# Second attention's probabilities and values as rows 124 to 127 of the text's keys and values, in a two-attention kernel on one core

## The chip, the core and the metric

The kernel runs on one core of a Trainium2 chip, in float32. The metric is the device time of one execution in microseconds (us). Below, PE is the matrix engine, DVE the vector engine, ACT the scalar engine, POOL the GpSimd engine, and SP the engine whose queue issues nearly all DMAs here.

## What is computed

The inputs are `x` (2 x 2048 x 640) and a context of 2 x 128 tokens of 384 channels. The first 124 tokens are text, the last 4 are called `ca`. There are 8 heads of 80 channels.

```
query = x @ Wq;  keyt = enc @ Wk;  valt = enc @ Wv          # 124 keys
hs = mha(query, keyt, valt)
ca_q1 = einsum('btc,th->bch', ca, Wq_ca)                      # 384 rows per batch
ca_q1 = ca_q1[:, linspace(0, 383, 2048).astype(int), :]       # 2048 rows, each row 5 or 6 times
ca_hs1 = mha(ca_q1, x, x)                                     # 2048 keys
ca_hs2 = mha(ca_hs1 @ Wq, ca @ Wk_ca, ca @ Wv_ca)             # 4 keys
out = (hs + ca_hs2) @ Wout + b_out + x
```

`mha` is softmax attention with the scale 80 ** -0.5. The second attention has only 384 different query rows per batch, since the 2048 rows repeat them in runs. Its last step has 4 keys: for each of the 384 rows and 8 heads there are 4 probabilities, `p2`.

## The kernel before, in words

**Order.** The work is written as tasks: Python generators that yield steps (`Do`) with an engine, a function, the events that it waits for, the buffers that it takes and frees, and the events that it marks. The tasks are started at lines 2151 to 2180. The literal `Desk.ORDER` (lines 74 to 152) lists task numbers; `Desk.run` (line 183) replays it, and each entry issues the next step of that task. A suffix a, v or g on an entry puts the step on ACT, DVE or POOL. Each engine and SP's queue execute in exactly this order, so an instruction that waits holds all that stand behind it on its engine.

**Helpers.** Nearly all matmuls have the profile's line L211 (`matmul`), warm-up matmuls L215, transposes L219, all operations of DVE, ACT and POOL L226, SP's DMAs L236, and the indirect additions L1971. `matmul` issues a product either whole (the row says 128*128) or as four strips of 32 output columns (128*32), which run beside each other. A float32 product takes two passes, so the profile counts 32 instructions for 16 strips.

**Stages.** Names in parentheses are those of the profile.

- Front: loads of x, Wq and the context; queries of block 0 (`queries`, line 1072, pq), keys (`keys`, line 800, pk), text values (`text_values`, pv into the tiles `vpad`, one per batch, 128 rows x 8 heads x 96), the second attention's values times Wout (`values_weights`, line 904, pw into w2_sb, with the bias b_out as its last row), and the table of row indices (`gather_rows`, line 859, query).
- Eight blocks of 512 rows of x: queries (`queries` while the block number is under FAST = 2, otherwise `queries_fast`, line 1173, which forms seven products of sums of x and Wq, x_sums and wq_sums), and the adapter's operands (`yz_block`, pyz).
- Adapter, once for each batch (`adapter`, line 1498): scores against 2048 rows (s), maxima on DVE (mx), exponentials on ACT (ea), and the contraction (`contract`, acc).
- Second attention, once for each batch (`second`, line 1657): the 384 x 8 x 4 probabilities are written into a padded tile (p2pad), turned on PE (pt_p), copied (p2T), multiplied with w2 (po<-w_sb,p2T, 6 products for each batch, copied to o2 by ACT) and stored as a 384 x 640 tensor in HBM (o<-o).
- Text attention in 16 units of 256 rows: scores (`text_scores`, sc, with the last query rows from a trip through HBM, first_rests and rests), softmax (p), a 32x32 transpose on DVE (eb), a trip through HBM (kept) from which pT comes back with the keys in its rows, in four parts of 32 rows (`probabilities`, line 1859), products with the values (`hidden`, ph), sums of those (hs) and products with Wout (`text_out_fast`, line 2004, po). Each po is added on DVE to the residual rows (x_more, last_rows), which were loaded from x (`residual`, line 1949) into one of eight row tiles.
- End of a row tile (`stored`, line 2117): once its four adds are done, POOL adds the rows of o2 to it by an indirect DMA with addition (`add_second`, line 1969), then it is stored. Units of batch 0 that are done before o2 is known are stored to HBM (early) and loaded again later. For the last unit the indirect addition is made ahead of the adds.

In rows 124 to 127 of `vpad` stand zeros, and pT's rows 124 to 127 hold the padding of p.

Of the kernel before, what the change touches and what calls it, by code (L numbers as in the profile page):

```python
# [8 lines left out]
F32 = mybir.dt.float32  # L9
# [7 lines left out]
T = 4  # L17
# [49 lines left out]
class Desk:  # L67
# [7 lines left out]
        2 2 2 2 0 4 4 108 109 110 2 2 0 0 0 0 0 0 0 0 0 2 2 2 2 2 0 4 4 0 4 2 2 0 0 37 111 113a 112a 4 4 0 0 115a 116a  # L75
        114v 4 6 6 6 5 5 6 6 6 2 16 16 16 16 16 16 16 5 3 6 16 16 13 11 11 7 5 3v 3 9 3a 6 6 7 117v 3 119v 3a 7 3 6 8
        118v 120v 1 9 8 8 6 122v 8 7 9 121 123a 124 7 8 7 7 8 7 126v 125v 6 7 7 127v 7 7 6 128a 129v 7 7 7 6 130a 131v
        132a 8 16 8 133 133 9 16 16 16 16 37 8 16 133 133 8 9 134 8 133 8 9 8 140 12 11 19 19 19 135 19 137 37 15 9 9
        9 9 15 15 15 15 15 15 15 136 9 136 136 136 9 15 15 19 19 19 19 19 136 19 10 18 9 9 9 138 9 10 13 18 12 18 37
        12v 12 13 18 18 12 37 15 37 143v 37 10 12 13 19 142v 19 19 19 19 18 37 13 37 12a 144a 9 145a 13 12 12a 146v 13  # L80
        14 102 102 107 136 136 141 141 141 141 141 6 136 136 107 139 18 18 37 40 18 37 37 147a 18 148 148 102 37 148
        148 102 102 102 139 139 22 139 139 22 22 22 22 22 139 17 17 149a 148 148 148 17 17 17 17 17 139 150 18 37 18
        44 18 18 150 17 17 150 37 17 17 151 102 37 150 22 22 22 18 18 151 37 148g 148 37 152a 151 151 150 139 139 151
        22 18 153 153 153 20 153 22 151 153 153 22 22 20 20 20 21 102 20 21 44 154 155 155 148 159g 160g 162g 161g 20
        158 158 151 151g 37 22 158 22 164 102 20 20 164 151 23 155 158 163 166 21 168a 163 166 37 169a 163 170a 171 20
        37 164 164 164 164 102 164 165 163 40 37 165 25 25 155 25 155 25 25 25 151 172a 20 173 173 20 174 37 164g 24
        158 173 173 155 155 173 173 164 21 23 37 167 156 23 23 155 164 48 37 175 173 173g 177 177 37 37 173 167 21 37
        167 177 155 177 177 177 48 37 177 21 37 178 179 179 23 157 25 157 157 157 157 157 25 25 158 180 21 25 24 37
        179 179 180 180 180 183g 177g 181g 182g 157 157 185 24 24 37 24 179 157 191a 185 180 179 192a 173 186 25 23 25
        23 177 180 187 187 187 187 193 177 52 179 37 25 37 195 195 37 24 185 179g 196 195 195 196 196 196 187 187 187  # L90
        196 25 179 179 197a 23 196 189 37 185 189 190 195 195 202a 195 37 25 203 56 204 195g 184g 205 23 205 195 37 37
        150 187 141 141 141 187 205 205 205 23 205 188 190 188 190 52 37 194 26 206 207 24 28 194 194 194 28 27 27 28
        28 195 28 194 28 28 28 28 158 23 208 205 213 214 37 37 214 27 208 208 208 208 217a 208 176 37 209g 211g 210g
        205g 205 218 28 141 205 176 141 215 37 215 216 219a 220a 208 208g 212g 37 176 28 56 28 221 28 221 208 37 213
        221 222a 221 221 216 213 216 37 37 223 213 221 221 224 28 28 30 194 194 194 194 30 176 198 199 176 158 208 150
# [144 lines left out]
def kernel(  # L240
# [30 lines left out]
    G = 32  # L271
    ONE = Y + T
    MAX = 4 * T
    VH = 2 * R
    VR = D - VH
    UNITS = B * NST // 2
    FAST, SPARE, IDLE = 2, 0, 14
    N2 = 3 * G + 2 * B * T

    desk = Desk(tc)  # L280
    matmul, transpose, copy, dma = desk.matmul, desk.transpose, desk.copy, desk.dma
    EITHER = ("ACT", "DVE")

# [1926 lines left out]
```

## Time and profile before

| | us |
|---|---|
| median of 3 runs | 583.91 |
| lowest and highest of the 3 | 580.39, 592.51 |
| the profiled execution's own time | 588.51 |
| its span in the profile | 586.7 |
| mean granted PE clock over the span | 0.988 |

The profiled execution is thus one of its own, 4.6 us above the median of the three runs. Busy times in it: DVE 394.1, ACT 265.8 and POOL 185.2 us; PE is shown with the prediction. The DMA engines move 115.27 MB, 196 GB/s in the mean, 10.69 MB of it on POOL's queue (the indirect additions and small loads).

How to read the rows: a group's row has the line, the engine, the operation, the tile written and the tiles read (buffer numbers left out), the partitions and elements, and the count; then the busy time in us, the mean duration of one in ns (on PE this is the latency, since matmuls are pipelined), and the engine's idle time just before them with what ended it. A row of the chain has the start, the duration in us, and the instructions that ran without a gap. A window's row has its length, then busy time and instructions of PE, PE's weight loads, DVE, ACT and POOL, then the granted PE clock (1.00 is full), the busy share of the DMA engines and GB/s.

### The profile page before, as it was taken

To read this page: it belongs to the slowest core of one execution; us is meant where nothing else is said; L and a number is where in the kernel's file an instruction comes from. 1 tells how busy PE (TensorE), PEld (TensorE's weight loads), DVE (VectorE), ACT (ScalarE), POOL (GpSimd) and SP (SyncE) were. 2 spreads that over 40 slices of the span, in tenths; PEclk is the share of its full clock that TensorE was granted. 3 is DMA by queue.
4 is the path that set the end of the run, shared out by engine and by line. 5 is a ranking of instruction groups with operands and counts; after the bars stand their busy time and mean duration, and the time that the engine had idled before them with its cause. 6 is when DMAs were issued, how large, how long until landed. Compare 5 with 4: busy or idle time off the path is not lost.

```text
span 586.7 us, 18285 instructions
## 1 busy us (share of the span) xinstructions
PE 572.0 (97%) x7769; PEld 307.1 (52%) x7769; DVE 394.1 (67%) x642; ACT 265.8 (45%) x738; POOL 185.2 (32%) x231
## 2 busy tenths in 40 slices
PE   9999899999999999999999999999999999997997
PEld 7563335546556645555454454555555565553453
DVE  2377799999997855579899999746334433652343
ACT  2011255555446788997344352585887411000100
POOL 7103051154232270012151335315323340442261
PEclk9999999999999999999999999997999999999799
DMA  8997585744898658445659989999868997999895
GB/s 273 173 249 153 110 165 138 164 122 141 155 247 166 204 153 184 118 135 159 194 166 192 260 259 247 243 248 250 235 177 204 216 239 224 216 214 232 258 201 171
DMA packets 153418, 115.27 MB, mean 196 GB/s; under 512 B 83317, under 2 KB 125685, under 8 KB 153338
## 3 DMA queue, kind: packets, MB, share of 16 engines
q1 hardware_dynamic: 147706, 103.42, 67.9%
q0 software_dynamic: 5632, 10.69, 10.7%
q8 instruction: 61, 1.00, 0.8%
q14 instruction: 19, 0.16, 0.1%
HBM read 72.54 MB, written 41.53 MB: 194 GB/s over the span
## 4 chain that ended last, share of the span: by engine, by line
PE 86%; DVE 6%; SPq 2%; ACT 2%; DMA 2%; issue 2%; DVEq 0%; ACTq 0%
PE po L211 28%; PE pq L211 23%; PE acc L211 7%; PE sc L211 7%; PE ph L211 6%; PE s L211 6%; SPq L236 2%; PE pyz L211 2%; DVE mx L226 2%; PE pk L211 1%; DMA xi<-in_x_dram 1%; PE unread L215 1%; DMA kept<-eb 1%; ACT ea L226 1%; ACT p L226 1%
## 5 line engine op out<-in xcount | busy, mean ns | idle before, releaser
L226 DVE TENSOR_REDUCE mx<-s 128x4 f32<-128x2048 f32 x48 | 109.0, 2271 | 4.8 <-PE s L211 4.7
L226 ACT ACTIVATE ea<-s 128x2048 f32<-128x2048 f32 x48 | 90.7, 1890 | 34.9 <-PE s L211 33.6
L226 ACT ACTIVATE p<-sc,m 128x124 f32<-128x124 f32 x256 | 89.9, 377 | 27.9 <-DVE m L226 27.7
L226 POOL TENSOR_TENSOR p<-p,r 128x992 f32<-128x992 f32 x25 | 48.8, 1954 | 157.9 <-DVE r L226 137.7
L211 PE MATMUL pq<-xt,wq_sb 128*32 128x256 f32 (+3 forms) x962 | 84.6, 427 | 0.1
L211 PE MATMUL po<-wout_sums,hs 128*32 128x320 f32 (+1 forms) x952 | 80.3, 442 | 0.0
L211 PE MATMUL po<-wout_sb,hs 128*32 128x320 f32 (+1 forms) x934 | 80.0, 438 | 0.2 <-ACT p L226 0.2
L226 DVE TENSOR_TENSOR x_more<-x_more,po 128x320 f32<-128x320 f32 x68 | 31.7, 479 | 54.8 <-PE po L211 54.7
L226 ACT ACTIVATION_READ_ACCUMULATOR p<-sc,m 128x1 f32 x256 | 56.1, 219 | 0.0
L226 ACT COPY hs<-ph 128x512 f32<-128x512 f32 (+1 forms) x27 | 14.7, 561 | 85.6 <-PE ph L211 85.5
L211 PEld LDWEIGHTS pq<-xt,wq_sb 128*32 128x32 f32 (+1 forms) x962 | 35.0, 113 | 33.9 <-issue 18.3
L211 PE MATMUL ph<-pT,vpad 128*32 128x256 f32 x768 | 48.1, 385 | 4.4 <-issue 4.4
L211 PEld LDWEIGHTS po<-wout_sb,hs 128*32 128x32 f32 (+1 forms) x934 | 34.7, 113 | 32.6 <-issue 2.9
L211 PE MATMUL acc<-ea,y_sb 128*32 128x384 f32 (+2 forms) x768 | 51.5, 389 | 0.0
L211 PEld LDWEIGHTS po<-wout_sums,hs 128*32 128x32 f32 (+1 forms) x952 | 34.4, 114 | 31.8 <-issue 3.1
L226 DVE TENSOR_REDUCE m<-sc 128x4 f32<-128x496 f32 x64 | 40.5, 659 | 10.9 <-PE sc L211 10.7
L226 DVE TENSOR_TENSOR last_rows<-last_rows,po 128x320 f32<-128x320 f32 x60 | 28.1, 481 | 28.3 <-PE po L211 27.8
L226 DVE STREAM_TRANSPOSE eb<-p 128x1024 f32<-128x1024 f32 x32 | 39.5, 1234 | 4.2 <-DMA kept<-eb 4.1
L1971 POOL DMA_INDIRECT last_rows<-o,query x16 | 25.1, 1570 | 53.7 <-DVE last_rows L226 50.6
L226 POOL TENSOR_TENSOR hs<-hs 128x256 f32<-128x256 f32 x32 | 26.8, 904 | 42.8 <-ACT hs L226 20.4
L211 PEld LDWEIGHTS sc<-kmain,q 64*128 64x128 f32 x512 | 32.4, 189 | 14.9 <-issue 8.8
L1971 POOL DMA_INDIRECT x_more<-o,query x16 | 25.6, 1599 | 45.2 <-ACT p L226 17.3
(210 smaller groups left out, 796.1 us busy)
## 6 DMA issues: line engine op xcount, KB each, us to landing
kept<-eb SPq DMA_DIRECT2D x32, 512.0 KB, 5.0
pT<-kept SPq DMA_DIRECT2D x64, 256.0 KB, 6.1
landing<-away SPq DMA_DIRECT2D x60, 128.0 KB, 3.4
xi<-in_x_dram SPq DMA_DIRECT2D x28, 256.0 KB, 4.6
x_more<-in_x_dram SPq DMA_DIRECT2D x17, 320.0 KB, 5.5
out_dram<-last_rows SPq DMA_DIRECT2D x16, 320.0 KB, 5.2
out_dram<-x_more SPq DMA_DIRECT2D x16, 320.0 KB, 5.2
last_rows<-in_x_dram SPq DMA_DIRECT2D x15, 320.0 KB, 4.9
```

What stands on the lines that cost most here:

```text
L211: self.pin(self.nc.tensor.matmul(out[strip], lhsT[:, strip], rhs, **kw))
L215: self.pin(self.nc.tensor.matmul(out, zeros, zeros, start=True, stop=True))
L226: return lambda *args, **kw: self.pin(getattr(engine, what)(*args, **kw))
L236: self.pin(self.nc.sync.dma_start(out, in_))
L1971: desk.pin(nc.gpsimd.indirect_dma_start(out=t, out_offset=None, in_=o2_of[b], in_offset=bass.IndirectOffsetOnAxis(ap=query[:, st : st + 1] ...
```

## The change

1. **Values.** `values_weights` becomes `second_values`: no transposes, no spreading, no product with Wout. The four values per head (vca) are copied from PSUM and written by eight small DMAs on SP into rows 124 to 127 of both vpad tiles (event "v2").
2. **Probabilities.** In `second`, the normalized p2 (p2t) is multiplied on PE with rows of 0 and 1 that POOL builds (`rows_of_tokens`, 3 memsets and 6 affine_selects for each batch): output column t takes the probabilities of the second-attention row that belongs to row t of x. The product has 32 rows (4 tokens x 8 heads) and 2048 columns, four groups of 512 side by side in one PSUM bank, in 6 matmuls. Two copies bring it to SBUF, one DMA on SP to HBM (p2, 256 KB, pieces of 128 bytes; event ("o2", b)).
3. **Text.** pT's last part has 28 rows in place of 32, and a fifth DMA on SP (`second_rows`, 32 KB) writes rows 124 to 127 from p2, for each of the 16 units. ph waits for all five parts and for "v2".
4. **What goes.** The index table, the o2 product with its copies, stores and 32 indirect additions, the early stores (4) and reloads.
5. **Bias.** b_out is loaded as a 128 x 640 tile; each of the 32 row tiles gets it by an addition of 128 x 640 before its po adds, 20 of them on POOL and 12 on DVE.
6. **Stores.** A row tile is stored after its four adds; those of the last unit in two halves of 320 columns.
7. **Front and order.** FAST goes from 2 to 1, so block 1's queries take the seven-product form. The first loads have another order (rows 0 and 1 of x, the first part of Wq, rows 2 and 3, the rest), and block 0's first query product is split into two halves of 256 columns. The key products have 248 columns in place of 256. 14 warm-up matmuls move from the first 9 us to just before the first sc. The whole literal `ORDER` is new: in it the first ph of a batch stands behind that batch's p2 product, where before the first ph stood ahead of the p2 transposes of batch 0.

On the engines this changes the number of instructions so: ACT loses 14 copies (o2, p2T) and those of w2; SP has 433 DMAs in place of 419; POOL's additions of two tiles in SBUF go from 57 to 81 (20 bias, 5 more of x_sums, 4 more of hs, the rest unchanged in kind), while its 32 indirect additions go.

The diff, without `ORDER` and cut to its core:

```diff
-    FAST, SPARE, IDLE = 2, 0, 14
+    FAST, SPARE, IDLE = 1, 0, 14
...
-    w2_sb = const.tile([N2 + 1, H], F32, name="w2_sb")
-    p2pad = const.tile([P, NCC, P], F32, name="p2pad")
-    query = const.tile([P, NST], mybir.dt.uint32, name="query")
+    bias = const.tile([P, H], F32, name="bias")
...
+        for op in (row(0), row(1), wq_rows(0), row(2), row(3)):
+            yield op
...
-                        pk[:, : B * NTOK], k_of(cc, c), ctxT[:, cc, :, :].rearrange("p b t -> p (b t)"),
+                        pk[:, : B * NK], k_of(cc, c), ctxT[:, cc, :, :NK],
...
-            dma(w2_sb[N2:, :], b_out[None, :])
+            dma(bias, b_out.partition_broadcast(P))
...
+        def away():
+            for b in range(B):
+                for g in range(4):
+                    k0 = G * g + T * b
+                    dma(vpad[b][NK:, 2 * g : 2 * g + 2, :], vca[k0 : k0 + T])
...
+        yield Do("SP", away, ["vca", "vpad"], marks=["v2"])
...
-            for i in range(NCH):
+            for u in range(2):
+
+                def part(u=u):
+                    for c in range(3):
+                        matmul(
+                            pq[c][:, 2 * P * u : 2 * P * (u + 1)], wq_of(0, c), t[:, 2 * u : 2 * u + 2, 0, :],
+                            start=(u == 0), stop=False, skip_group_check=True,
+                        )
...
+    def rows_of_tokens(b):
...
+            def steps(t=op.value[:, lo:hi], c=c, lo=lo, hi=hi):
+                desk.g_memset(t, 1.0)
+                for factor, base in ((1, NUM * lo - DEN * P * c), (-1, DEN * P * c - NUM * lo + DEN - 1)):
+                    desk.g_affine_select(
+                        out=t, in_=t, compare_op=ALU.is_ge, fill=0.0, base=base,
+                        pattern=[[factor * NUM, hi - lo]], channel_multiplier=-factor * DEN,
+                    )
...
+        def product(s):
+            pt = bank(s[0], f"pt_p2_{b}")
+            for g in range(4):
+                for c, (lo, hi) in enumerate(token_range):
+                    lo, hi = max(lo, 512 * g), min(hi, 512 * (g + 1))
+                    if lo < hi:
+                        matmul(
+                            pt[G * g : G * (g + 1), lo - 512 * g : hi - 512 * g],
+                            p2t[:, c].rearrange("p t h -> p (t h)"), by_token[b][0][:, lo:hi],
+                            start=True, stop=True, skip_group_check=True,
+                        )
+            return pt
...
+        p2_of[b] = hbm.tile([16, P, G], F32, tag=f"p2_{b}", name=f"p2_{b}")
+        yield Do(
+            "SP", lambda: dma(p2_of[b].rearrange("c p a -> p c a"), wide_p2.rearrange("p (c a) -> p c a", a=G)),
+            frees=[(eas, k)], marks=[("o2", b)],
+        )
...
+        def second_rows():
+            rows_in = p2_of[b].rearrange("(n c) (g t h) a -> g n t c (h a)", n=2, g=4, t=T)
+            dma(pT[NK:].rearrange("p i k h a -> p (i k) (h a)"), rows_in[n // 2, n % 2])
+
+        yield Do("SP", second_rows, [("o2", b)], marks=[("pT", m, 0)])
...
+        for k, (t, _, at) in enumerate(xr):
+
+            def add_bias(t=t):
+                (desk.g_tensor_tensor if desk.engine == "POOL" else desk.v_tensor_tensor)(t, t, bias, ALU.add)
+
+            yield Fork(one(Do(("DVE", "POOL"), add_bias, [at, ("wout", 2)], marks=[("xr", m, k)])))
...
-                "PE", product, [("pT", m), "v done"], needs=[(banks, 1)] + ([(hss, 1)] if c0 == 0 else []),
+                "PE", product, [("pT", m, j) for j in range(5)] + ["v done", "v2"], needs=[(banks, 1)] + ([(hss, 1)] if c0 == 0 else []),
...
-        if gather_last[m]:
-            op = yield Do("POOL", lambda: add_second(t, b, st), [*both, ("o2", b), "query"])
-            both = [op.at]
-        yield Do("SP", lambda: dma(rows_out, t), both, frees=[(rows, i)] + own)
+        cols = slice(0, H) if u == 2 else slice(u * HALF, (u + 1) * HALF)
+        yield Do(
+            "SP", lambda: dma(out[b, st * P : (st + 1) * P, cols], t[:, cols]), added,
+            frees=[(rows, i)] if u == 2 else [],
+        )
```

411 lines of the change are left out of this document (154 added, 257 removed).

## The prediction

> **What bounds the kernel now.** I read the page's busy table and chain first, then the list of what each engine waited for, then windows laid around the waits found, and last the SP queue's own timeline.
>
> ```profile
> span 586.7 us, 18285 instructions
> PE 572.0 (97%) x7769; PEld 307.1 (52%) x7769; DVE 394.1 (67%) x642; ACT 265.8 (45%) x738; POOL 185.2 (32%) x231
> ...
> PE 86%; DVE 6%; SPq 2%; ACT 2%; DMA 2%; issue 2%; DVEq 0%; ACTq 0%
> ```
>
> PE is busy 97% of the span and carries 86% of the chain, so only two things can move the end: PE work, and time in which PE waits or runs at half clock. The list of PE's waits is short:
>
> ```profile
> PE ph L211 <- issue: 4.4, 1, 4.4
> PE pv L211 <- DVE vpad L226: 2.5, 1, 2.5
> PE sc L211 <- DVE hs L226: 1.5, 1, 1.5
> ```
>
> Two of the three are followed by a slow clock (columns of a window: length, PE busy, ..., granted clock, DMA share, GB/s):
>
> ```profile
> 402.00:405.41 3.41, 3.41 (x34) 2.67 (x34) 1.43 (x3) 0.42 (x1) 2.61 (x2) 0.50 1.06 312
> 405.41:408.83 3.42, 3.42 (x36) 1.55 (x32) 0.49 (x2) 2.84 (x9) 0.00 (x0) 0.50 1.08 236
> 538.53:541.94 3.41, 0.46 (x8) 0.00 (x0) 0.33 (x1) 0.00 (x0) 0.00 (x0) 1.00 1.03 253
> 541.94:545.36 3.42, 1.96 (x20) 1.16 (x24) 0.00 (x0) 0.00 (x0) 0.00 (x0) 0.50 0.90 333
> 545.36:548.77 3.41, 3.41 (x28) 1.38 (x24) 0.82 (x2) 0.58 (x1) 0.72 (x1) 0.50 0.87 294
> ```
>
> Each slow stretch is two windows of 3.41 us at 0.50. In the first PE is busy throughout and loses 6.83 x 0.5 = 3.4 us. In the second it is busy 1.96 + 3.41 = 5.4 us and loses 2.7. With the waits themselves: 1.5 + 3.4 = 4.9 us near 400, and 4.4 + 2.7 = 7.1 us near 540.
>
> The wait near 540 is made by SP's queue (start, length; POOL's timeline, SP's, then the chain):
>
> ```profile
> 517.11 1.54 POOL L1971 DMA_INDIRECT x_more<-o,query  x1 [0.30 <-issue]
> ...
> 527.40 0.83 SPq L236 DMA_DIRECT2D out_dram<-x_more  x2
> 534.78 0.34 SPq L236 DMA_DIRECT2D x_more<-in_x_dram  x1
> 535.17 0.43 SPq L236 DMA_DIRECT2D pT<-kept  x1
> ...
> 538.99 4.42 issue
> 543.40 1.94 PE ph L211 x16
> ```
>
> Finished rows get their second-attention part by two indirect additions (POOL, the second until 518.7), and only at 527.40 are they stored. The next row load takes their place at 534.78, the last part of pT is queued behind it at 535.17, and the ph product starts at 543.40.
>
> **PE work removed.** Prices are rows of the chain (start, us, count) and of the groups by form:
>
> ```profile
> 32.55 1.72 PE pq L211 x4
> 42.69 1.30 PE pk L211 x6
> 68.51 1.08 PE pw L211 x16
> 453.65 1.73 PE ph L211 x32
> 470.43 10.24 PE po L211 x38
> 504.74 12.92 PE po L211 x192
> ...
> L211 PE MATMUL po<-w_sb,p2T 113*32 113x320 f32 x72 | 6.6, 438 | 0.0
> L211 PE MATMUL po<-w_sb,p2T 113*128 113x320 f32 x6 | 2.1, 432 | 0.0
> L219 PE MATMUL pt_p<-ident,p2pad 128*113 128x128 f32 x6 | 1.0, 283 | 0.1
> ```
>
> A strip of 320 columns costs 12.92/192 = 67 ns, a full product 10.24/38 = 269 ns. The o2 products go: 72 x 67 + 6 x 269 = 6.5 us. The two pw products go, 16 strips each: 32 x 67.5 = 2.2. The p2 transposes with those of the values: 0.9. The first block's key products shrink from 256 to 248 columns, 30 full-size equivalents x 217 x 8/256 = 0.2.
>
> Block 1's queries become the seven-product form that other blocks have. Plain they are 25 products, each of two passes at 430 ns, 21.5 us. The new form has 56 + 16 passes over 256 columns at 216.5 (1.73/32 = 54 for a strip, as ph's) and 10 of 512 at 430: 19.9. That saves 1.6.
>
> Added are two p2 products of 32 rows, each some 2048 columns in four 32-row strips. Side by side a strip of 512 costs 430/4 = 108 ns a pass, so 0.9 us a product; one behind another 3.4. I take 0.9 twice, as the strips in these rows run side by side: 1.7. Sum: -6.5 - 2.2 - 0.9 - 0.2 - 1.6 + 1.7 = **-9.7** (-4.6 if serial).
>
> **The stall near 540.** Without an indirect addition a row's store needs only DVE's adds, and x_more's were done before the second indirect addition began, 10 us ahead of 527.40. Row loads and pT parts then stop queueing behind it: **-7.1**. What is late next is the fifth part of pT, below, but there it was available long before.
>
> **Other engines.** POOL loses 32 indirect additions (half of them in the first row) and gets bias additions, priced by the second:
>
> ```profile
> L1971 POOL DMA_INDIRECT last_rows<-o,query x16 | 25.1, 1570 | 53.7 <-DVE last_rows L226 50.6 <-issue 1.5 <-DMA last_rows<-early 1.4
> L226 POOL TENSOR_TENSOR wout_sums<-wout_sb,wout_sums 128x640 f32<-128x640 f32 x2 | 3.1, 1556 | 0.2
> ```
>
> Of 32 bias additions POOL has 20 at 1.56 us, 31 us; DVE has 12. POOL's 0/1 rows are two sets of nine operations over some 680 columns, at most 1.56 each by the same row, and need nothing of p2. POOL at 32% and DVE at 67% have the room in the sum, so I take 0 for it; the cover is that rows are loaded well ahead of their po sums. Without that cover one late addition costs PE 1.56. ACT loses 14 copies and gains 4. The indirect additions, the o2 tensor and the early rows (some 14 MB by their sizes) leave the DMA engines: 0 while PE is not short of data, and a gain only inside the waits below.
>
> **New waits.** Every ph product now waits for a fifth part of pT, and that for p2 (DMA issues with us to landing; one tile's instructions with ns min/median/max):
>
> ```profile
> pT<-kept SPq DMA_DIRECT2D x64, 256.0 KB, 6.1
> landing<-away SPq DMA_DIRECT2D x60, 128.0 KB, 3.4
> xi<-in_x_dram SPq DMA_DIRECT2D x28, 256.0 KB, 4.6
> z<-zs SPq DMA_DIRECT2D x8, 256.0 KB, 3.2
> away<-first_rests SPq DMA_DIRECT2D x2, 256.0 KB, 3.2
> first_rests<-away SPq DMA_DIRECT2D x4, 128.0 KB, 3.3
> ...
> L226 ACT CAST first_rests<-pq x2: 374/376/378, 41.1 to 42.1; 128x256 fp32r<-128x256 f32 x2
> L226 ACT CAST rests<-first_rests x2: 619/620/622, 70.0 to 70.5; 128x512 fp32r<-128x512 f32 x2
> ```
>
> The chain behind the p2 product: two ACT copies of 256 columns, 0.8; the 256 KB store, between 3.2 (z<-zs) and 4.6 (xi, 128-byte pieces); the 32 KB load, between 3.3 and 6.1. That is 7.3 to 11.5; I take 7.5 to 8.5, as the load is small. Before its own first ph the new instruction order has 5.2 us of PE work for batch 0 (scores, yz) and 6.0 for batch 1: **+2.2** (0 to 5) and **+2.4** (0 to 7; batch 1 falls where DMA is over 0.9). Behind a waiting fifth part on SP stand the next row loads and stores, so this wait is not refunded elsewhere.
>
> At the start, the first sc in the new order stands directly behind the values' products, where before block 1's queries stood between. It needs the first block's last query rows: evacuation 0.8, store 3.2, load 3.3, two casts 1.2 = 8.5 us. Beside it lies 5.4 us of PE work, and ahead of the load SP has about 3 us of other issues (eight small value parts among them). That is a wait of 6, less the 2.5 at pv that it covers: **+4** (0 to 7). The warm products, moved there from the start, fill this idle time and add none.
>
> Half clock behind these waits: of the three waits shown two drew a slow stretch. One of 3.4 us with even odds: **+1.7** (0 to 7). The rule beside these rows is in the Trainium skill, "TensorE: Matmul & The Clock Gate", Part 1: the clock is halved after at least one idle window of about 3.4 us. The trace's slow windows have that length, but the one at 402 followed only 1.5 us of idle. By the rule, none of waits this short would slow the clock, and the sum would be 575.3.
>
> **The tail.**
>
> ```profile
> 583.22 0.33 SPq L236 DMA_DIRECT2D out_dram<-x_more  x1
> ```
>
> The span ends 3.5 us behind the issue of the last store of 320 KB. The last unit is now stored in halves; its gain lies between 0 and 0.5 (landing's 128 KB took 3.4 as well, z<-zs 3.2), I take **-0.3**.
>
> **Sum**: -9.7 - 7.1 + 2.2 + 2.4 + 4 + 1.7 - 0.3 = -6.8. The profiled execution took 588.5, so it would be 581.7; that execution is 4.6 above the median of 583.9, so the forecast against the median is 577.1, put at 577.0.
>
> **The rivals.** (a) The new waits are hidden. The chain times are medians of a loaded DMA system, now 14 MB lighter, and 5.2 to 6 us of cover stands against 7.5. Then only -9.7 - 7.1 - 0.3 = -17.1 counts: 566.8. Against it: z<-zs alone took 3.2 from issue to landing, twice in a row that is 6.4 without copies.
>
> (b) Slower. One mechanism: POOL's additions hold up DVE's sums of two SBUF tiles.
>
> ```profile
> 398.23 3.02 DVE L226 TENSOR_TENSOR hs<-hs 128x256 f32<-128x256 f32 x1 [0.20 <-ACT hs L226]
> ...
> 398.52 2.44 POOL L226 TENSOR_TENSOR p<-p,r 128x992 f32<-128x992 f32 x1
> ```
>
> This hs sum took 3.02 us beside a POOL addition, and PE's sc waited for it: the 4.9 us near 400. Such POOL additions rise from 57 to 81. From 577.0 to the 2% bound at 595.6 is 18.6 us, four such events that reach PE; it gives 597. Against it: one of 32 sums reached PE before. The Trainium skill, "SBUF — State Buffer", section "Who interferes with whom", says a DVE instruction with two SBUF inputs and a GpSimd one that reads SBUF lock each other out for a whole instruction; the 3.02 agrees.
>
> (c) Batch 1's adapter chain, not PE, sets when p2 is known. Then the 9 us of PE work saved before it turn into a wait at its first ph, and with that wait's 2.4 in it: 577.0 + 9 - 2.4 = 583.6. For it: DVE, which has the score maxima mx, is on the chain at 6%. Against it, PE's waits for mx:
>
> ```profile
> PE s L211 <- DVE mx L226: 0.4, 2, 0.2
> ```
>
> **How the numbers follow.** My forecast 0.53, (a) 0.27, (c) 0.14, (b) 0.06. The bounds of 2%, about what a measurement tells from no change, are 572.2 and 595.6. Faster: most of (a), 0.25, and 0.05 of the forecast's low end, 0.30. Slower: (b), 0.06. Same: 0.64. The range 566 to 588 leaves out (b), the lower part of (a) and a little of (c). The likeliest case by itself spans 570 to 585.
>
> **What would show it.** L1971 gone from the groups; no PE idle time near the end. A PE wait of 2 to 3 us before the first ph of each batch, ended by a DMA into pT; none means (a). A wait of 3 to 6 us before the first sc. PE busy down by 9 to 12 us. hs sums on DVE of 2 us and more beside POOL's additions mean (b). A gap at batch 1's p2 product that DVE ends means (c). I am wrong on the sum if the slow stretches are more than two, or if a wait appears where none of these parts puts one.

## The result and the profile after

The kernel after takes **592.88 us** (median of 20 runs, 587.82 to 596.48) against 583.45 (20 runs) for the kernel before: ratio 1.0165, 95% interval 1.0134 to 1.0197. It is slower by 9.4 us; I had forecast 577.0, 6.5 faster. The profiled execution took 594.39, 1.5 above the median.

The page of the kernel after (span, busy times, shares of the chain):

```profile
span 592.5 us, 18520 instructions
PE 562.9 (95%) x7934; PEld 308.1 (52%) x7934; DVE 405.7 (68%) x643; ACT 262.3 (44%) x729; POOL 181.9 (31%) x208
...
PE 77%; DVE 12%; DMA 5%; issue 2%; ACT 2%; SPq 2%; ACTq 0%; DVEq 0%
```

PE is busy 9.1 us less, as forecast (9 to 12), and yet the span is 5.8 longer: PE's share of the chain fell from 86% to 77%, and DVE's and DMA's rose. PE waits more. PE's longest waits in the kernel after:

```profile
PE pt_x L219 <- DMA xz<-in_x_dram: 5.6, 2, 4.1
PE ph L211 <- DMA pT<-p: 5.0, 1, 5.0
PE sc L211 <- ACT rests L226: 4.6, 1, 4.6
PE po L211 <- DVE x_more L226: 3.1, 2, 3.0
PE ph L211 <- issue: 2.9, 1, 2.9
PE s L211 <- DVE mx L226: 1.8, 2, 1.2
```

The first is the start, where the warm products stood before. The two waits at ph (batch 0, batch 1) and that at sc are those that I had named. The one at po, 3.0 us, nobody had. Windows of the kernel after tell what they cost; the first three are all its stretches at half clock in which PE works:

```profile
65.70:72.53 6.83, 4.21 (x40) 2.52 (x44) 6.59 (x9) 3.52 (x16) 3.63 (x3) 0.50 1.02 194
318.29:321.70 3.41, 2.73 (x28) 1.58 (x32) 0.00 (x0) 0.58 (x1) 1.84 (x2) 0.50 0.49 115
328.53:335.36 6.83, 5.74 (x44) 2.16 (x48) 4.82 (x8) 2.09 (x10) 2.09 (x2) 0.50 0.83 188
300.00:340.00 40.00, 32.08 (x420) 16.27 (x420) 29.03 (x38) 12.28 (x46) 16.75 (x13) 0.87 0.72 168
480.00:520.00 40.00, 36.94 (x576) 21.49 (x572) 23.04 (x43) 5.05 (x20) 7.27 (x7) 1.00 0.77 197
520.00:580.00 60.00, 60.00 (x944) 30.39 (x940) 27.43 (x57) 4.04 (x8) 18.77 (x18) 1.00 0.54 151
```

and the last three of the kernel before:

```profile
300.00:340.00 40.00, 39.59 (x535) 20.70 (x527) 39.66 (x49) 16.05 (x63) 14.71 (x14) 1.00 0.89 217
480.00:520.00 40.00, 40.00 (x623) 20.15 (x625) 18.70 (x36) 4.06 (x9) 14.65 (x13) 1.00 0.82 211
520.00:580.00 60.00, 55.58 (x824) 28.28 (x820) 23.10 (x52) 3.96 (x8) 21.28 (x16) 0.94 0.97 231
```

The end is as forecast: from 520 to 580 PE has no idle time and the full clock. Most of the loss is from 300 to 340: PE is busy 7.5 us less there, and of its busy time 2.73 + 5.74 us ran at half clock, which loses half of them, 4.2 us: 11.7 in all. From 480 to 520 it is 3.1.

What happens from 305 to 336 is seen in the timelines of the kernel after: SP's queue, then PE, then DVE (start, length, what; in brackets the idle time ahead and what ended it):

```profile
309.56 0.38 SPq L236 DMA_DIRECT2D p<-rows  x1
...
312.69 0.43 SPq L236 DMA_DIRECT2D pT<-kept  x1
...
313.83 0.46 SPq L236 DMA_DIRECT2D pT<-p  x1
...
321.14 0.43 SPq L236 DMA_DIRECT2D z<-zs  x1
...
307.65 1.07 PE L211 MATMUL pt_p<-rows,p2t 128*32 128x512 f32 x12
318.97 3.25 PE L211 MATMUL ph<-pT,vpad 128*32 128x256 f32 x32 [4.95 <-DMA pT<-p]
...
329.62 4.50 PE L211 MATMUL po<-wout_sums,hs 128*32 128x320 f32 x32 [2.95 <-DVE x_more L226]
...
327.78 0.01 DVE L226 LOAD_MASK_SELECT zs<-yz  x1 [2.66 <-DMA z<-zs]
...
329.00 0.47 DVE L226 TENSOR_TENSOR x_more<-x_more,po 128x320 f32<-128x320 f32 x1
```

The store of p2 (p<-rows) is issued at 309.56, the fifth part of pT (pT<-p) at 313.83, with six other DMAs issued in between, and ph begins at 318.97, 10.3 us behind the end of the product (308.72). Behind that, z<-zs is issued only at 321.14; DVE, which works in its own order, waits 2.66 us for it and adds x_more behind it; PE's po waits 2.95 us for that addition. Both waits are followed by slow PE work: 32 products take 3.25 and 4.50 us, where the same take 1.93 and 2.36 in no_block below.

What SP's queue itself waited for, in two stretches of the kernel after (300 to 330, 470 to 490):

```profile
SPq L236 <- ACT rows L226: 9.0, 1, 9.0
...
SPq L236 <- DMA away<-wq_sums: 4.0, 1, 4.0
...
SPq L236 <- ACT rows L226: 5.8, 1, 5.8
SPq L236 <- DMA out_dram<-x_more: 4.5, 1, 4.5
SPq L236 <- DMA p<-rows: 1.9, 1, 1.9
```

"ACT rows" is the copy of p2 from PSUM. SP reached the store 9.0 us (batch 0) and 5.8 us (batch 1) before that copy was made, and until then it issued nothing.

The 4.0 us follow from the 9.0. The store of wq_sums (away<-wq_sums) stands behind the store of p2 and was issued at 313.21, against 308.10 in no_block; the part of pT at 318.89 waits until it has landed, and z<-zs stands behind that part. Its data was there at 317.01, so SP held z<-zs back by 4.1 us. From its issue until DVE went on it then took another 6.6 us (2.5 in no_block), beside what SP had issued just ahead of it.

### The profile page after: what moved, and what is told of

The parts are those of the page before. It is cut to its first block, busy times and chain, and to the rows that moved or that the text cites. A ratio compares the mean times of both kernels' runs of the same rounds, so it can differ in the third digit from the quotient of the medians.

```text
span 592.5 us, 18520 instructions
## 1 busy us (share of the span) xinstructions
PE 562.9 (95%) x7934; PEld 308.1 (52%) x7934; DVE 405.7 (68%) x643; ACT 262.3 (44%) x729; POOL 181.9 (31%) x208
## 4 chain that ended last, share of the span: by engine, by line
PE 77%; DVE 12%; DMA 5%; issue 2%; ACT 2%; SPq 2%; ACTq 0%; DVEq 0%
PE po L211 25%; PE pq L211 19%; PE acc L211 7%; PE ph L211 7%; PE sc L211 6%; PE s L211 6%; DVE mx L226 5%; SPq L236 2%; PE pyz L211 1%; PE pv L211 1%; DMA z<-zs 1%; PE pk L211 1%; DVE xt L226 1%; DMA xz<-in_x_dram 1%; DMA away<-wq_sums 1%
## 5 line engine op out<-in xcount | busy, mean ns | idle before, releaser
L226 DVE TENSOR_REDUCE mx<-s 128x4 f32<-128x2048 f32 x48 | 109.4, 2278 | 10.4 <-PE s L211 10.1
L226 POOL TENSOR_TENSOR p<-p,r 128x992 f32<-128x992 f32 x25 | 46.6, 1863 | 157.0 <-DVE r L226 157.0
L211 PE MATMUL po<-wout_sums,hs 128*32 128x320 f32 (+1 forms) x940 | 80.7, 445 | 3.1 <-DVE x_more L226 3.1
L211 PE MATMUL po<-wout_sb,hs 128*32 128x320 f32 (+1 forms) x970 | 78.9, 433 | 0.0
L211 PE MATMUL pq<-xt,wq_sb 128*32 128x256 f32 (+3 forms) x936 | 75.7, 402 | 0.0
L226 POOL TENSOR_TENSOR hs<-hs 128x256 f32<-128x256 f32 x36 | 28.2, 792 | 132.0 <-DVE hs L226 91.3
L211 PE MATMUL ph<-pT,vpad 128*32 128x256 f32 x768 | 47.9, 388 | 7.8 <-DMA pT<-p 5.0
L211 PEld LDWEIGHTS po<-wout_sums,hs 128*32 128x32 f32 (+1 forms) x940 | 35.4, 115 | 36.1 <-issue 3.7
L211 PEld LDWEIGHTS pq<-xt,wq_sb 128*32 128x32 f32 (+1 forms) x936 | 36.9, 117 | 28.3 <-issue 11.9
L211 PEld LDWEIGHTS po<-wout_sb,hs 128*32 128x32 f32 (+1 forms) x970 | 34.6, 111 | 31.3 <-issue 1.7
L211 PE MATMUL acc<-ea,y_sb 128*32 128x384 f32 (+2 forms) x768 | 49.6, 382 | 0.0
L226 ACT COPY hs<-ph 128x512 f32<-128x512 f32 (+1 forms) x24 | 12.3, 528 | 66.6 <-PE ph L211 66.6
L211 PEld LDWEIGHTS ph<-pT,vpad 128*32 128x32 f32 x768 | 25.9, 112 | 24.9 <-issue 10.8
L211 PE MATMUL pq<-xt,wq 128*32 128x512 f32 x308 | 38.8, 596 | 0.0
L211 PEld LDWEIGHTS sc<-kmain,q 64*128 64x128 f32 x512 | 31.1, 187 | 11.4 <-issue 9.2
```

Source lines behind the costliest of these rows:

```text
L211: self.pin(self.nc.tensor.matmul(out[strip], lhsT[:, strip], rhs, **kw))
L226: return lambda *args, **kw: self.pin(getattr(engine, what)(*args, **kw))
```

## The experiments

Four causes stood against one another: the wait of ph for p2's trip through memory (theory 1 in the expectations); POOL and DVE burdened by bias additions (rival (b), theory 2); the wait at the first sc (theory 3); and SP's queue, which the store of p2 holds up in order, with all that stands behind it (theory 4). In `ORDER`, 310 and 443 are `second` of batch 0 and 1, 311 and 444 `rows_of_tokens`, 68 and 88 the first text units of the two batches, 140 the first rests, 11 the small loads of values. Ratios are to the kernel before, in runs of the same chip. In kernels with a changed `ORDER` the lines are one lower (L210 for L211).

### Is it the dependence on p2, the additions, or the front?

**rows_free**: no unit waits for p2; the fifth part is a load of x of the same size, so the output lacks the second attention.

```diff
-            rows_in = p2_of[b].rearrange("(n c) (g t h) a -> g n t c (h a)", n=2, g=4, t=T)
-            dma(pT[NK:].rearrange("p i k h a -> p (i k) (h a)"), rows_in[n // 2, n % 2])
+            rows_in = x[b, : T * HEADS, : HEADS * R].rearrange("(t c) k -> t c k", t=T)
+            dma(pT[NK:].rearrange("p i k h a -> p (i k) (h a)"), rows_in)
```

> The changed kernel, except that the fifth part of pT is read from x, which is there from the start, so no ph product waits for p2 (the second attention's share of the output is left out; the DMA keeps its size and its place in SP's queue, and p2 is still made and stored). Theory 1 (the trip of p2 through memory is what costs): the waits of 5.0 us at 313.5 and 2.9 us at 484.3 go, with the half clock behind the first (about 1.7 us) and part of the 3.0 us wait at 326.2 that follows it; 581 to 585 us, ratio to the kernel before 0.995 to 1.002. Theory 2 (the bias additions on POOL and DVE cost): these waits are only filled by others, at most 4 us less, 589 us or more. Theory 3 (the front is what costs): 588 to 590.

591.59 us, ratio 1.0135 (1.0085 to 1.0184). Two rows, one of what SP's queue waited for, one of PE's waits, in rows_free:

```profile
SPq L236 <- ACT rows L226: 9.0, 1, 9.0
```

```profile
PE ph L211 <- DMA pT<-in_x_dram: 5.5, 1, 5.5
```

The fifth part, now a plain load of x, came as late as before (4.2 us behind the store's issue, 4.3 in the kernel after), since SP still stood 9.0 us at the store. The dependence alone is not the cause.

**no_bias**: no bias is added, and the output lacks it.

```diff
-            yield Fork(one(Do(("DVE", "POOL"), add_bias, [at, ("wout", 2)], marks=[("xr", m, k)])))
+            yield Fork(one(Do(("DVE", "POOL"), lambda: None, [at, ("wout", 2)], marks=[("xr", m, k)])))
```

> The changed kernel without the 32 additions of the bias tile (the bias is left out of the output; every other instruction keeps its place). Theory 2: the 3.0 us wait at 326.2 goes with its half clock of 2.2 us, and smaller delays of DVE and POOL with it; 583 to 587 us, ratio 1.000 to 1.006. Theories 1 and 3: 591 to 594 us, ratio 1.013 to 1.018, as the additions lie beside PE work and the wait at 326.2 comes from the SP queue and the mask shuffle that waits for it on DVE.

592.79, 1.0158 (1.0105 to 1.0212), with the same waits. Rival (b) falls. Its own sign, hs sums on DVE of 2 us and more, is missing in the kernel after, too: there is none, where the kernel before had the one of 3.02 us.

**front_sp**: the small loads of values stand behind the loads of the first rests.

```diff
-  18 9 11 9 139 ... 135 106 140 0 140 141 140 140 140 18
+  18 9 9 139 ... 9 9 140 140 140 140 140 11 9 144v ... 135 106 0 141 18
```

> The changed kernel with one edit of the order: the trip of the first block's last query rows (store, the returns of the key parts, loads of first_rests) stands ahead of the eight small value DMAs in SP's queue. Theory 3: these eight issues (5.2 us) are what the first sc waits for; its wait falls from 4.6 us to under 1, and the half clock behind it (about 2 us) goes; 586 to 589 us, ratio 1.004 to 1.010. If the values' rows, now later, hold up the tiles that take the place of the front's (yt, rests), the time stays at 592 to 594. Theories 1 and 2 say that PE only waits elsewhere: 590 to 593.

593.77, 1.0177 (1.0129 to 1.0225). In its profile the wait for the rests was 0.6 in place of 4.6, with full clock behind it, and the span 1.6 shorter; the median did not fall. The front is not where the 9 us are.

**before_again**: the kernel before, unchanged, for another profiled execution.

> The kernel before, unchanged, for a second profile. The 20 runs have a median of 583.5 us against 588.5 of the profiled one. If the two stalls that the prediction priced (7.1 us near 540, 4.9 us near 400) belong to every run, they show again. If they are events of that one execution, one or both are missing here and the time is 579 to 585 us; then the 7.1 us that the prediction took off was never there to be had.

584.58 us, span 582.8. A window and the wait behind it in before_again:

```profile
520.00:580.00 60.00, 56.16 (x868) 31.64 (x860) 24.69 (x56) 3.85 (x8) 21.40 (x16) 1.00 0.96 238
```

```profile
PE ph L211 <- issue: 3.0, 2, 2.6
```

The stall near 540 is there, but 2.6 us long and with no half clock. The 7.1 us that I had removed in the forecast were 4.4 and 2.7 in one execution, not in all. The hs sum near 400 again takes 3.09 us and PE waits 1.5 us for it, this time with no half clock behind it.

### The queue, and the dependence with it

**no_block**: rows_free, and the two stores of p2 (310, 443) stand later in SP's order, where their data exists. The output again lacks the second attention.

```diff
-        yield Do("SP", second_rows, [("o2", b)], marks=[("pT", m, 0)])
+        yield Do("SP", second_rows, [], marks=[("pT", m, 0)])
...
-  276 105 310 233 286 ... 34 286 335 341 ... 458 443a 443 88 88 ... 465v 80 451 80
+  276 105 233 286 ... 34 286 310 335 341 ... 458 443a 88 88 ... 465v 80 443 451 80
```

> As rows_free (the fifth part of pT read from x, so the second attention's share of the output is left out), and the store of p2 stands later in SP's queue, behind the parts of pT and the row loads that it stood ahead of. Theory 4: what ph waits for at 313.5 and 484.3 is the SP queue itself, since the store of p2 stands in it 9.0 and 5.8 us before its data is there and holds the last part of pT, the landing loads and the row loads behind it. Then both waits go here though they stayed in rows_free, with the half clock behind the first and the 3.0 us at 326.2: 10 to 14 us less than the changed kernel, 579 to 583 us, ratio 0.992 to 1.000. Rival (the adapter's maxima on DVE set the pace there, and PE would wait for them instead): the wait at 313.5 falls to under 1 us, but the time only to 588 to 590, ratio 1.008 to 1.012.

**580.21** (12 runs), ratio 0.9944 (0.9911 to 0.9977): 12.7 us under the kernel after. PE's timeline in no_block:

```profile
315.90 1.93 PE L210 MATMUL ph<-pT,vpad 128*32 128x256 f32 x32 [0.34 <-ACT yz L225]
...
322.92 2.36 PE L210 MATMUL po<-wout_sums,hs 128*32 128x320 f32 x32 [0.45 <-DVE x_more L225]
...
475.32 1.94 PE L210 MATMUL ph<-pT,vpad 128*32 128x256 f32 x32
```

The three waits are 0.34, 0.45 and nothing, and the wait at po, which has nothing to do with p2, went with them. The wait at the first sc (4.2) is still there. So the loss lies in p2's way through memory: the wait for it, and what it holds up.

### Whole computation, other orders on SP

Six kernels keep everything and only move entries of `ORDER`. **early_p2**: batch 0's shares and product 2.4 us earlier, its store behind the last part of pT; batch 1's product earlier too.

```diff
-  68 286 314a 245 295 245 307 306 274 310 317a 312 310 312 245 ... 311 311 311 310 310a ... 105 310 233 ... 456 461 444 444 444 443 456
+  68 286 310 314a 245 295 310 245 307 306 274 317a 312 312 311 311 311 310 245 ... 310a ... 105 233 ... 276 68 310 318 ... 80 88 444 444 444 443 452
```

> The whole computation of the changed kernel, with p2 known earlier: for batch 0 the probabilities are divided ahead of one maximum on DVE and the p2 product stands two query products earlier on PE (2.4 us), and its store behind the last part of pT in SP's queue; for batch 1 the product stands ahead of seven other products (5 us). Theory 4: the wait of 2.9 us at 484.3 goes, that of 5.0 at 313.5 falls to 1 to 3, the half clock behind it goes: 584 to 588 us, ratio 1.001 to 1.007. Rival (DVE's maxima set the pace): at most the 2.9 us of batch 1, 589 to 591, ratio 1.010 to 1.013.

592.87, 1.0166 (1.0132 to 1.0200). Batch 0's ph wait fell from 5.0 to 0.34, but the po wait was 3.0 again. Here SP did not hold z<-zs back: it was issued at 319.28, 0.03 us behind its data, but DVE got it only at 324.26, 5.0 us later against 2.5 in no_block. So a late issue is not the only way to that wait; I take the loads issued just ahead of it for the reason, which no run separates. (The profile puts the wait down to a bias addition of POOL, which ended at the same moment, 325.97, as DVE's addition of po, 325.95.) Batch 1's product stood too early, and PE waited 5.1 us for DVE's p2t: a fault of this edit.

**early_front** is early_p2 with the edit of front_sp.

> early_p2 with the edit of front_sp as well (the first block's last query rows ahead of the eight small value DMAs). If the front's 4 us reach the end once the middle no longer waits for the SP queue: 3 to 4 us less than early_p2, 581 to 585 us, ratio 0.996 to 1.002. If the front is always given back (as the median of front_sp by itself says): the same as early_p2 within 1 us.

592.33, 1.0159 (1.0122 to 1.0196).

**sp_only**: nothing but SP's order; the stores behind the last pT part, the first fifth part of batch 0 behind the next unit's loads.

```diff
-  105 310 233 ... 276 68 318 ... 48 68 315 48 264 46 46 327g ... 443a 443 88 88 86
+  105 233 ... 276 68 310 318 ... 48 315 48 264 46 46 68 327g ... 443a 88 443 86 88
```

> The whole computation of the changed kernel; only SP's queue is in another order. Batch 0: the store of p2 stands behind the last part of pT and the row load that it stood ahead of, and the fifth part of the first unit behind the next unit's loads. Batch 1: the last part of pT ahead of the store, one row load ahead of the fifth part. The chain of p2 itself is as long as before. Theory 4 (the blocked queue): the wait at 313.5 stays at 4 to 5 us, as ph still waits for the chain product, copies, store, load, but what stood behind it in SP's queue comes earlier, so the 3.0 us at 326.2 with its half clock goes: 586 to 590 us, ratio 1.004 to 1.011. Rival 5 (only the length of the chain of p2 counts): 591 to 594 us.

593.29, 1.0150 (1.0099 to 1.0201): the po wait went, and ph waited 7.5 us in batch 0 and 3.5 in batch 1. That is the time of its rival 5, by which only the length of p2's chain counts; act_trip and first_slice below try that length.

**batch0** (early_p2's edit of batch 0 with sp_only's place of the fifth part) and **both** (with batch 1's product three steps earlier, and sp_only's edit of batch 1); **both_front** adds that of front_sp.

> sp_only for batch 0 alone, and there the p2 product 2.4 us earlier as in early_p2 (the probabilities divided ahead of one maximum on DVE). Theory 4: the waits at 313.5 and at 326.2 are both under 1 us, as in no_block, while 2.9 us stay at 484.3: 8 to 10 us less than the changed kernel, 583 to 585 us, ratio 0.999 to 1.003. Rival 5: as early_p2 without its 5.2 us at batch 1, 587 to 589 us.

> batch0, and for batch 1 the p2 product ahead of one score product (2.6 us earlier, behind its probabilities' 472.6), with the last part of pT and one row load ahead of the store and of the fifth part. Theory 4: the 2.9 us at 484.3 go too; 580 to 582 us, ratio 0.993 to 0.999, the time of no_block with the whole computation. If it stays at batch0's time, the wait at 484.3 has another cause than the chain of p2.

> both, with the edit of front_sp. With nothing behind it that gives the time back, the front's 2 to 4 us should reach the end: 577 to 579 us, ratio 0.988 to 0.995. If the front is given back in any case, as the median of front_sp says: 580 to 582.

593.92 (1.0152, 1.0102 to 1.0202), 593.82 (1.0160, 1.0105 to 1.0215) and 593.82 (1.0154, 1.0105 to 1.0203). ph of batch 0 waits 7.0 to 7.5 in the four kernels from sp_only on. The fifth part now stands behind a part of pT that waits itself (2.8 us in batch0), and behind two row loads of 320 KB; from its issue to ph it takes 5.5 us in sp_only and 6.9 to 7.4 in the other three, 5.1 in the kernel after. None of the six kernels reached the time that theory 4 gave it: what one place gained came back at another. Every one has a PE wait of 5 us or more. Store and load, 9 to 10 us in sequence, stand in one queue with 26 other DMAs (305 to 336 in the kernel after).

### The trip on a queue of its own

**queues**: ACT issues the store, POOL the first fifth part of a batch; the products as in both (`ORDER` not shown here and below).

```diff
-            "SP", lambda: dma(p2_of[b].rearrange("c p a -> p c a"), wide_p2.rearrange("p (c a) -> p c a", a=G)),
+            "ACT",
+            lambda: desk.a_dma_start(p2_of[b].rearrange("c p a -> p c a"), wide_p2.rearrange("p (c a) -> p c a", a=G)),
...
+            (desk.g_dma_start if m in (7, 12) else dma)(
...
-        yield Do("SP", second_rows, [("o2", b)], marks=[("pT", m, 0)])
+        yield Do("POOL" if m in (7, 12) else "SP", second_rows, [("o2", b)], marks=[("pT", m, 0)])
```

> The whole computation, with p2's way through memory taken off SP: ACT issues the store right behind its copy, and POOL issues the first fifth part of each batch, behind a bias addition. The p2 products stand 2.4 us (batch 0) and 1 to 2 us (batch 1) earlier in PE's order. If what costs is that these two DMAs stand in SP's queue in order and hold up everything behind them, the ph waits fall from 5.0 and 3.0 to under 1.5 each, the 9.0 and 5.8 us waits of SP for ACT rows go, z<-zs is not late and the 3.0 us wait at po goes: the time is that of no_block plus what is left of the ph waits, 579 to 585, ratio 0.99 to 1.00. The wait of 4.6 at the first sc stays. Rival: the trip itself is what costs, from whatever queue it is issued (store and load land 4 to 7 us each): the ph waits stay at 4 us and more, half clock follows, and the time is 590 to 594. Against both: ACT or POOL is held up by its issue, seen as PE waiting for ACT or POOL around 310 or 480.

598.02 us (4 runs), 1.0233 (1.0184 to 1.0283), slower than all others. POOL's timeline in queues:

```profile
310.57 1.55 POOL L225 TENSOR_TENSOR wout_sums<-wout_sb 128x640 f32<-128x640 f32 x1 [13.59 <-PE pq L210]
...
316.68 3.02 POOL L225 TENSOR_TENSOR x_more<-x_more,bias 128x640 f32<-128x640 f32 x2
319.65 0.66 POOL L225 DMA_DIRECT2D pT<-p  x1
```

I had put the fifth part behind six additions of POOL, and it was issued at 319.65 although ACT had issued the store at 308.06; ph waited 9.6 us. The same fault as on SP, on another engine, made by me.

**act_trip**: ACT issues both, where it stood idle; batch 1's product stands 1.2 us earlier than in the kernel after. Against queues:

```diff
-        yield Do("POOL" if m in (7, 12) else "SP", second_rows, [("o2", b)], marks=[("pT", m, 0)])
+        yield Do("ACT" if m in (7, 12) else "SP", second_rows, [("o2", b)], marks=[("pT", m, 0)])
```

> The whole computation. As queues, but ACT issues both the store of p2 and each batch's first fifth part, at places where it stood idle for 6 us (batch 0) and 14 us (batch 1); batch 1's p2 product stands 1.2 us earlier. If only the place in an in-order queue costs: batch 0 store at 308, landed at 312 to 313, fifth part landed at 316 to 317, ph wait 1 to 2.5; batch 1 ph wait under 3; SP waits for no ACT rows; po wait under 1; time 580 to 587, ratio 0.993 to 1.005. If the trip is too long to be hidden: ph waits of 4 us and more in one batch or both, with half clock, and 589 to 595. The wait at the first sc stays at 4 to 5.

591.32 (6 runs), 1.0129 (1.0082 to 1.0176). ACT's and PE's timelines in act_trip:

```profile
310.73 0.39 ACTq L225 DMA_DIRECT2D p<-rows  x1
315.55 0.51 ACTq L225 DMA_DIRECT2D pT<-p  x1
...
470.41 0.39 ACTq L225 DMA_DIRECT2D p<-rows  x1
478.09 0.27 ACTq L225 DMA_DIRECT2D pT<-p  x1
...
319.82 1.93 PE L210 MATMUL ph<-pT,vpad 128*32 128x256 f32 x32 [2.27 <-ACT p L225]
...
482.88 3.64 PE L210 MATMUL ph<-pT,vpad 128*32 128x256 f32 x32 [3.27 <-DMA pT<-p]
```

SP waits for no copy of p2 any more, and the po wait is 0.33. ACT itself stood 8.0 us in batch 1 until the store had landed, which no PE wait shows. But the store alone took 4.8 and 7.7 us until the load could follow, and the load another 4 to 5; ph waited 2.3 and 3.3, the second with half clock behind it (3.64 for 32 products). Together with 1.8 us that my earlier shares made PE wait for q, that is most of the 10.4 by which its span exceeds no_block's. So the dependence costs without the blocking, too: rows_free had the blocking without the dependence, act_trip the dependence without the blocking (and the 1.8 us), and each keeps the time at 591. Their costs don't add up: with both it is 593.

**act_trip_front** adds the edit of front_sp.

> The whole computation. As act_trip, and in SP's queue the eight small loads of values stand behind the loads of the first rests, so that the wait at the first sc falls from 4.6 to under 1.5. If the front's wait counts in full, 3 us under act_trip; by what front_sp showed (wait gone, median the same), within 1.5 us of act_trip.

592.22, 1.0137 (1.0086 to 1.0188), no clear difference from act_trip. Here the wait at the first sc was 5.9 us in the profile, against 3.0 in act_trip: the edit alone does not set it. Over all profiles of kernels without the edit it lies between 1.7 and 6.0, with it between 0.6 and 5.9.

### A shorter trip

**first_slice**: as act_trip, but the 32 KB of p2 that the first unit needs are stored by a DMA of their own, ahead of the whole, and loaded from there; the shares keep their old place.

```diff
+        own = wide_p2[G * (n // 2) : G * (n // 2 + 1), 256 * (n % 2) : 256 * (n % 2 + 1)]
+        yield Do(
+            "ACT",
+            lambda: desk.a_dma_start(first_of[b].rearrange("c p a -> p c a"), own.rearrange("p (c a) -> p c a", a=G)),
+            marks=[("o2 first", b)],
+        )
...
+            if n == FIRST[b]:
+                rows_in = first_of[b].rearrange("c (t h) a -> t c (h a)", t=T)
```

> The whole computation. As act_trip, but the slice of p2 that the first unit of the batch needs (32 of 128 rows, half the columns, 32 KB) is stored by a DMA of its own ahead of the whole p2, and the first fifth part is loaded from it; batch 0's shares keep their old place in ACT's and DVE's order, so that the 1.8 us wait for q that act_trip had goes. If the length of the trip is what is left: slice landed in 2.5 to 4 us in place of 4.8 and 7.7, ph waits under 1.5 us in both batches, no half clock from them, time 579 to 585, ratio 0.992 to 1.003. If the loss comes back elsewhere: 588 to 593, with another PE wait of 3 us and more between 310 and 500. The wait at the first sc stays at 3 to 5.

**583.63** (12 runs), ratio 0.9970 (0.9941 to 1.0000). ACT's and PE's timelines in first_slice:

```profile
308.94 0.35 ACTq L225 DMA_DIRECT2D p2f<-rows  x1
309.33 0.49 ACTq L225 DMA_DIRECT2D p<-rows  x1
312.33 0.51 ACTq L225 DMA_DIRECT2D pT<-p2f  x1
...
466.64 0.32 ACTq L225 DMA_DIRECT2D p2f<-rows  x1
...
472.42 0.26 ACTq L225 DMA_DIRECT2D pT<-p2f  x1
...
316.35 1.93 PE L210 MATMUL ph<-pT,vpad 128*32 128x256 f32 x32 [1.18 <-DMA pT<-p2f]
...
476.99 1.93 PE L210 MATMUL ph<-pT,vpad 128*32 128x256 f32 x32 [0.87 <-DMA last_rows<-in_x_dram]
```

The slice lands in 3.4 us, and within 5.8 in batch 1; the waits are 1.2 and 0.9 and the clock stays full behind them. With the whole computation kept, 9.3 us of the loss are back. Against act_trip two things changed, the slice and the place of the shares, which had cost 1.8 us there.

**first_slice_front** adds the edit of front_sp.

> The whole computation. As first_slice, with the eight small loads of values behind the loads of the first rests in SP's queue. The wait at the first sc falls below 3; by front_sp and act_trip_front this moved the median by under 1.5 us, and I expect the same here: within 2 us of first_slice.

581.90 (12 runs), ratio 0.9983 (0.9946 to 1.0020), span 580.3: no clear difference from the kernel before, nor from first_slice. These two are the best versions with everything computed; the change then costs nothing, and brings nothing that is sure. The PE work saved doesn't show in the time: PE is busy 5.0 us less in first_slice than in before_again (562.0 against 567.0), with 3.4 us lost to half clock in it, and idle 4.5 us more (20.3 against 15.8), nearly all of it at the start, which is taken up below.

## Why the prediction was wrong

**PE work removed, -9.7: right.** Half of PE's busy time at half clock counts as lost, not as work. PE's work is then 572.0 - 6.1 = 565.9 us in the profiled execution of the kernel before, 567.0 in before_again (no half clock), and 562.9 - 6.3 = 556.6 in the kernel after: 9.3 or 10.4 less. The p2 products ran side by side, 12 strips in 1.07 us (307.65).

**The stall near 540, -7.1: mis-sized.** It went, as said. But the 4.4 and the 2.7 were those of one execution; before_again shows 2.6 and full clock. And the sum then took off another 4.6 us for that execution's offset to the median. Part of the offset was this very stall, so some of it was counted twice. The 4.9 us near 400, which the prediction priced but left in the sum's base, are not in the kernel after.

**Batch 0's first ph, +2.2 (0 to 5): this step failed.** Measured are 11.7 us from 300 to 340. Two things are in it. The wait itself is 5.0: I priced the chain behind the product at 7.5 to 8.5 us, and it took 10.3, within the 7.3 to 11.5 that I had written and not believed. The store took 4.3 until the fifth part was issued, and the load, which I took for short since it is small, 5.1 until ph. The rest, 6.7 us, is the wait at po, for which the sum had nothing, and the half clock behind both waits. I said that "behind a waiting fifth part on SP stand the next row loads and stores", and drew from it only that the wait is not refunded. I never asked what stands behind the *store*, which waits longer (9.0 us) and earlier. The late z<-zs, DVE's wait, the po wait of 3.0 and the slow stretch behind it follow from that; no_block, which takes the dependence and the blocking away, has none of them. The Trainium skill, "DMA: Bandwidth & Descriptors", section "Anatomy of one DMA — SWDGE (gpsimd) path", notes that DMA engines don't wait for semaphores, that the wait happens on the issuing sequencer ahead of the dispatch. The 9.0 us in which SP issued nothing agree.

**Batch 1's first ph, +2.4 (0 to 7): right in size**, 2.9. The SP queue stood 5.8 us there, and the store took 5.1 us until the fifth part could be issued at 484.73.

**The first sc, +4 (0 to 7): too low, within its range.** PE's timeline there, in the kernel after:

```profile
59.22 3.39 PE L215 MATMUL unread<-zeros 128*128 128x128 f32 x28
62.54 1.16 PE L211 MATMUL sc<-kmain,q 64*128 64x124 f32 x16
68.32 1.11 PE L211 MATMUL sc<-krest,rests 64*128 64x124 f32 x8 [4.62 <-ACT rests L226]
```

The wait of 6 that I had worked out had the warm products (unread) in it as filling. So it is to be held against 3.4 + 4.6 = 8.0 us, less the 2.5 at pv: +5.5. The list of PE's waits hides this, since the 3.4 us appear at the start, where the warm products stood before and PE now waits 5.6 us in place of 1.1, while its useful work starts no later (block 0's first query product at 9.32 against 9.38). I can't say what the front is worth at the end: the wait varies by 4 us from one profiled kernel to the next with nothing changed there, and in five pairs of kernels that differ by the edit of front_sp no median moved by more than its uncertainty.

**Half clock, +1.7 (0 to 7): too low.** There are three stretches, behind waits of 5.0, 4.6 and 3.0 us, where I had allowed for one of 3.4 us with even odds; PE lost half of 4.21 + 2.73 + 5.74 us in them, 6.3. The rule set beside it, by which waits as short as forecast draw none, would have given less still.

**The tail, -0.3: right in sign.** The span ends 2.8 us behind the last store's issue (589.75), in place of 3.5.

**The rivals.** (a), waits hidden, is what first_slice comes near to, after a change of mine, and then at 583.6 us and not at the 566.8 of (a). (b) is excluded by no_bias. (c) is not seen: no gap at batch 1's p2 product that DVE ends, in the kernel after. The slower case that came was none of them: my rival on that side had the wrong engine.

With the terms as measured, from the span of before_again (582.8) to that of the kernel after (592.5): -10.4 (PE work), +6.3 (half clock), and PE idle for 29.6 us in place of 15.8, +13.8. Of these, +5.0 and +3.0 are batch 0's waits at ph and po, +2.9 batch 1's at ph, +4.5 the start and +2.2 the first sc (4.6 in place of 2.4 at pv), -3.0 the stall near 540 with a small wait at ph beside it, -3.4 three waits that are gone (1.5 and 0.6 at sc, 1.3 at po), -0.7 the tail. The 3.3 us left are waits of at most 1.2 us each.

## What to carry to other kernels

A store that is issued from an in-order queue costs in two ways: its consumer waits for the trip, and everything behind it in the queue waits for its data. Each alone kept the time at 591 here. So before a result is sent through memory, look at what stands behind its two DMAs, and price the trip by its upper bound if the cover is thin. If the trip can't be hidden, issue it from an engine that is idle there, and send first, by itself, the piece that the first consumer needs; the rest has time. A stall seen in one profiled execution is worth a second execution before it enters a sum, and not once more through the offset to the median. And products that only fill a wait cost nothing where they stand, but where they are moved to they hide how long the hole there is.

## What the runs showed of the hardware

- The same 256 KB store in pieces of 128 bytes took 4.8 us from issue to the next issue behind it in batch 0 of act_trip and 7.7 in batch 1; 32 KB of it, in the same pieces, 3.4 and 5.8 in first_slice. The 32 KB load behind it took from its issue to ph 4.0 us in first_slice, 5.1 in the kernel after and, behind two row loads of 320 KB, 5.5 to 7.4 (sp_only, batch0, both, both_front). I can't say which part is the pieces and which the other traffic.
- Half clock followed PE waits of 5.0, 4.6 and 3.0 us (after) and 3.3 (act_trip), and at the first sc also waits of 1.7 (sp_only, at half clock from 67.8 to 71.2) and 2.0 (first_slice, from 67.6 to 71.0); it did not follow 2.9 (after, batch 1), 2.3 (act_trip) and 2.6 (before_again). The same wait of 1.5 us for the hs sum near 400 was followed by two windows of it in the profiled execution of the kernel before and by none in before_again. So the length of one wait doesn't tell it. The Trainium skill, "TensorE: Matmul & The Clock Gate", Part 1, names at least one idle window of about 3.4 us; by that rule the shorter ones would have cost nothing, and these runs show otherwise.
- The wait at the first sc, 60 us into the kernel, differs from one profiled kernel to the next by up to 4 us with the same code around it (1.7 in sp_only, 6.0 in rows_free).
